# LayerNorm of a mixture-of-experts layer: a ring of four row tiles, gamma in PSUM, part of the gates on GpSimd

## The chip, the cores and the metric

The kernel runs on one core of one Trainium2 chip. A core has five engines that run side by side, each with its own instruction queue: TensorE (PE, matrix products, with weight loads shown as PEld), VectorE (DVE), ScalarE (ACT), GpSimd (POOL) and SyncE (SP, which here only issues DMAs). SBUF is the on-chip memory of 128 partitions, PSUM the small memory that TensorE writes. The metric is the device time of one execution in microseconds (us); the median of several runs is compared. A profile is the record of one execution.

## The reference

Two layers over images of 32 x 128 channels x 56 x 56, all in float32. The first is a depthwise 7x7 convolution, a LayerNorm over channels, and a mixture of 8 experts with top-2 routing and a capacity; the second is a coordinate attention with a 3x3 convolution. The diff touches the LayerNorm, the logits and the gates:

```python
x = conv_general_dilated(input, dw_kernel, ..., feature_group_count=C) + dw_bias
x = transpose(x, (0, 2, 3, 1))
mu = x.mean(-1, keepdims=True)
var = x.var(-1, keepdims=True)
x = (x - mu) / sqrt(var + 1e-06) * ln_gamma + ln_beta
xf = x.reshape(T, C)                       # T = 32*56*56 = 100352 tokens, C = 128
logits = xf @ Wg + bg                      # E = 8 experts
topv, topi = top_k(logits, 2)
wts = softmax(topv, axis=-1)
order = argsort(-wts[:, 0])                # a token's priority
# each expert takes at most CAP tokens, in that order; gelu MLP; two results per token, weighted
out1 = input + x_skip + layer_scale * moe_out
# second layer: coordinate attention, 3x3 convolution, SiLU
```

## The kernel before

The program runs in four stages, one after the other on the same core.

1. Depthwise convolution as banded matrix products (L165), written to the DRAM buffer `y_d`.
2. LayerNorm, logits, top-2 and gates (L194 to L349). This is the stage that the diff changes.
3. Routing per expert (a search for the threshold of the capacity, from L448 and L452 on, mostly DVE), then gather (L657), the expert's MLP (L678 to L688) and scatter (L717).
4. The second layer: combine (L973), attention, convolution (L1056 to L1068).

Stage 2 works on 16 pairs of images. A pair has 49 tiles of 128 tokens (`TPP = 49`), and is handled as two units: 24 tiles (h = 0) and 25 tiles (h = 1, `U = 25`). For a unit, `centre` (L293) does per group of three tiles: three matmuls with `proj`, which subtract the mean and also give 8 logit columns (L310, tile `lnps` in PSUM, a pool of 8), a copy of the 136 columns by ACT into the tile `cen` (L311, a pool of 4), and squares by ACT. Where a tile is squared alone (all of h = 0) the activation also sums it into `var` (L315, an activation and a read of the accumulator); otherwise three tiles are squared at once into `sqs` (L317, one buffer), and DVE sums them in one reduce (L322). `spread` (L319) makes `rstd` from `var` by two POOL instructions (L323, and the power L324). `normalise` (L326 on) scales each tile by `rstd` and gamma on DVE into the row tile `xn` (L331; 137 columns: 128 of the token, 8 gates, 1 mark; a pool of 2) and scales the logits (L333).

Once both units of a pair are there, `top` (L234) finds the two largest logits of each token by a chain of DVE instructions of 392 elements (L237 to L250) and two small ones (L251, L252), `exp` (L254) is one ACT instruction, and `gates` (L257) makes w0 and w1 (L261 to L265), the gate columns of the row (L267 to L269), the mark (L270), and the priorities `prio` (L272, L274), all on DVE; then SP issues the store of the whole row tile, 3.36 MB, to `acc_d` (L276). The same queue issues the load of the next pair's `lnyt` (L298, two buffers).

In the source the stage is a loop over k (L337 to L349): unit k is centred while unit k-2 is normalised, and the pair two behind gets its `top` (odd k) or `exp` and `gates` (even k). A scheduler then sets the order of each engine's instructions; dependencies between engines become semaphore waits. Stage 3 begins on DVE with L452, which reads `prio`, and ACT's queue issues a fill of part of `acc_d` with zeros (L648, four DMAs of 13.4 MB).

Of the kernel before, what the change touches and what calls it, by code (L numbers as in the profile page):

```python
# [21 lines left out]
E = 8  # L22
CAP = int(1.25 * T / E)
FF = 4 * C
P = 128
# [22 lines left out]
def moe_conv_then_coordatt_kernel(ctx: ExitStack, tc: tile.TileContext, a: dict, out: bass.AP):  # L48
# [145 lines left out]
    with ExitStack() as st:  # L194
# [3 lines left out]
        xp = st.enter_context(tc.tile_pool(name="lnx", bufs=2, reuse_waits="tile"))  # L198
        sp = st.enter_context(tc.tile_pool(name="lns", bufs=3, reuse_waits="tile"))
        pp = st.enter_context(tc.tile_pool(name="lnp", bufs=8, space=PSUM))  # L200
        halves = ((0, TPP // 2), (TPP // 2, TPP))
        U = TPP - TPP // 2
        NSQ = TPP // 2
# [17 lines left out]
        class Pair:  # L221
# [5 lines left out]
            def tile(self, pool, tag, shape=None):  # L227
                return pool.tile(shape or [P, TPP], F32, tag=tag, name=f"{tag}{self.i}", bufs=2 if pool is xp else 1)

            def open(self):  # L230
                self.row = self.tile(xp, "xn", [P, TPP, RW])
                self.l = self.tile(sp, "lgs", [P, TPP, E])

            def top(self):  # L234
# [4 lines left out]
                self.oh = [self.tile(sp, f"oh{k}", [P, TPP, E]) for k in range(2)]  # L239
# [17 lines left out]
            def gates(self):  # L257

                n, mx, w0, w1 = TPP, self.m[1], self.tile(sp, "w0"), self.tile(sp, "w1")
                t = self.tile(sp, "gt", [P, TPP, E])  # L260
# [6 lines left out]
                nc.vector.tensor_tensor(row[:, :, C : C + E], oh[0], over_experts(w0, n), ALU.mult)  # L267
                nc.vector.tensor_tensor(t, oh[1], over_experts(w1, n), ALU.mult)
                nc.vector.tensor_tensor(row[:, :, C : C + E], row[:, :, C : C + E], t, ALU.add)  # L269
                nc.vector.scalar_tensor_tensor(row[:, :, C + E : RW], self.later.unsqueeze(2), -1.0, all_e.unsqueeze(2),  # L270
                                               ALU.mult, ALU.add)
                nc.vector.tensor_tensor(oh[1], oh[0], oh[1], ALU.add)  # L272
                cols = slice(self.i * TPP, (self.i + 1) * TPP)
                nc.vector.tensor_tensor(prio[:, :, cols].rearrange("p e t -> p t e"), oh[1], over_experts(w0, n), ALU.mult)  # L274
# [5 lines left out]
        class Unit:  # L280
# [12 lines left out]
            def centre(self):  # L293
# [7 lines left out]
                self.cen = self.tile(cp1, "cen", [P, U, C + E])  # L301
                self.var = self.tile(sp, "var")
                self.alone = 0 if self.h else NSQ
                if self.alone < self.n:
                    self.sq = qp.tile([P, U, C], F32, tag="sqs", name=f"sqs{self.nm}")
                for g in range(0, self.n, 3):
# [4 lines left out]
                    nc.scalar.copy(self.cen[:, g : g + m, :], ps[:, 0:m, :])  # L311
                    if g < self.alone:
                        for j in range(m):
                            sq = sp.tile([P, C], F32, tag="sq", name=f"sq{self.nm}_{g}_{j}", bufs=1)
                            nc.scalar.activation(sq, ps[:, j, 0:C], AF.Square, accum_out=self.var[:, g + j : g + j + 1])  # L315
                    else:
                        nc.scalar.activation(self.sq[:, g : g + m, :], ps[:, 0:m, 0:C], AF.Square)  # L317

            def spread(self):  # L319
                self.rstd = self.tile(sp, "rstd")  # L320
                if self.alone < self.n:
                    nc.vector.tensor_reduce(self.var, self.sq[:, 0 : self.n], AX.X, ALU.add)  # L322
                nc.gpsimd.tensor_scalar(self.var, self.var, 1.0 / C, 1e-6, ALU.mult, ALU.add)  # L323
                nc.gpsimd.tensor_tensor(self.rstd, self.var, bc(mhalf, [P, self.n]), ALU.pow)  # L324

            def normalise(self):  # L326
                pair = pairs[self.i]
                if self.h == 0:
                    pair.open()
                for j in range(self.n):  # L330
                    nc.vector.scalar_tensor_tensor(pair.row[:, self.j0 + j, 0:C], self.cen[:, j, 0:C],  # L331
                                                   self.rstd[:, j : j + 1], gamma_bc, ALU.mult, ALU.mult)
                nc.vector.tensor_tensor(pair.l[:, self.j0 : self.j1, :], self.cen[:, :, C : C + E],  # L333
                                        over_experts(self.rstd, self.n), ALU.mult)

        units = [Unit(i, h) for i in range(NPAIR) for h in range(2)]
        for k in range(len(units) + 3):  # L337

            pair = pairs[(k - 3) // 2] if k >= 3 else None
            if k < len(units):  # L340
                units[k].centre()
            if pair and k % 2 == 0:
                pair.exp()
            if k < len(units):
                units[k].spread()
            if 2 <= k <= len(units) + 1:
                units[k - 2].normalise()
            if pair:
                (pair.top if k % 2 else pair.gates)()  # L349
# [801 lines left out]
```

## Time and profile before

| what | time |
|---|---|
| median of 5 runs | 4330.45 us (4323.46 to 4344.73) |
| the profiled execution's own time | 4335.32 us |
| its span, first to last instruction | 4333.6 us |
| stage 1, until the last write of `yt` (L181) | about 613 us |
| stage 2, first matmul of L310 to the end of the last L274 | 632.3 to 1107.1 us |
| stage 3, first L452 to the last scatter of L717 | 1107.1 to 3134 us |
| busy over the whole span: PE, DVE, ACT, POOL | 3473.2, 2528.5, 1446.2, 2763.9 us |

The stores of L276 show the rhythm of stage 2: they are issued at 705.03, 732.50, 759.95, 787.41, 814.88, 842.35, 869.81, 897.27, 924.73, 952.19, 979.64 and 1007.11 us, 27.46 or 27.47 us apart.

How to read the rows: a line such as "L331 DVE SCALAR_TENSOR_TENSOR xn<-cen,rstd,gamma_bc 128x128" names the line of the kernel, the engine, the operation, what is written from what, and the size (partitions x elements). Line numbers "before" are those of the listing above; the changed kernel has its own, a few higher.

### The profile page before, as it was taken

How to read it: one execution, taken by the hardware profiler on the slowest of the kernel's cores; microseconds unless marked ns; L12 is line 12 of the kernel's file. 1: busy time of each engine (PE TensorE's matmuls, PEld its weight loads, DVE VectorE, ACT ScalarE, POOL GpSimd, SP SyncE). 2: the span in 40 equal slices, each digit the busy share in tenths (PEclk: the TensorE clock that was granted, in tenths of full speed). 3: DMA queues.
4: the chain of work that ended last, by engine and by line, in shares of the span. 5: the costliest groups of instructions: out<-in, count | busy, mean ns of one | idle time of the engine just before them, and what ended most of it. 6: DMA issues, size and time to landing. Idle time of an engine off the chain costs nothing. (4 is left out here: it accounts for less than half of the span.)

```text
span 4333.6 us, 61146 instructions
## 1 busy us (share of the span) xinstructions
PE 3473.2 (80%) x21565; PEld 1960.5 (45%) x21565; DVE 2528.5 (58%) x5710; ACT 1446.2 (33%) x3123; POOL 2763.9 (64%) x2044
## 2 busy tenths in 40 slices
PE   7999979885068576678688669888769999999899
PEld 4644559885034232334343334444334444444444
DVE  3433328999948455775632112222268888888886
ACT  0000017664034343334344334445312333333332
POOL 5444414333048777677677567777779878787775
PEclk9999989776579787899899889999879999999999
DMA  9999985663991221111122122122165656555551
GB/s 177 177 178 183 191 171 213 246 246 157 320 297 43 51 62 46 51 44 53 51 56 57 50 55 57 57 57 57 53 220 163 201 166 196 181 186 188 166 165 72
DMA packets 678002, 580.88 MB, mean 134 GB/s; under 512 B 405848, under 2 KB 611184, under 8 KB 667248
## 3 DMA queue, kind: packets, MB, share of 16 engines
q1 hardware_dynamic: 411408, 319.81, 25.7%
q10 hardware_dynamic: 222816, 160.70, 14.3%
q0 software_dynamic: 43264, 94.64, 8.1%
q8 instruction: 184, 3.01, 0.3%
q14 instruction: 330, 2.70, 0.2%
HBM read 314.92 MB, written 260.09 MB: 133 GB/s over the span
## 5 line engine op out<-in xcount | busy, mean ns | idle before, releaser
L717 POOL DMA_INDIRECT acc_d<-yo,row x676 | 697.3, 1032 | 293.8 <-DMA acc_d<-yo,row 57.8
L1056 PE MATMUL pc<-v,wk 128*128 128x392 f32 x1920 | 702.7, 508 | 0.4 <-POOL v L1041 0.4
L678 PE MATMUL ph<-fxt,w 128*128 128x512 f32 (+1 forms) x1400 | 677.1, 627 | 5.7 <-ACT ht L679 5.7
L657 POOL DMA_INDIRECT xg_r<-acc_d,idx x556 | 560.5, 1008 | 182.8 <-issue 110.5
L686 PE MATMUL py<-ht,w 128*128 128x512 f32 (+1 forms) x1400 | 624.6, 589 | 0.0
L165 PE MATMUL acc<-xs,band 28*64 28x432 f32 (+2 forms) x11264 | 542.6, 532 | 59.2 <-issue 29.2
L679 ACT ACTIVATE ht<-ph,bias 128x512 f32<-128x512 f32 (+1 forms) x700 | 476.5, 682 | 246.0 <-PE ph L678 237.7
L1056 PEld LDWEIGHTS pc<-v,wk 128*128 128x128 f32 x1920 | 346.9, 191 | 306.9 <-issue 102.3
L165 PEld LDWEIGHTS acc<-xs,band 28*64 28x64 f32 x11264 | 311.7, 134 | 289.5 <-issue 193.8
L310 PE MATMUL lnps<-proj,lnyt 128*128 128x136 f32 x1568 | 364.8, 401 | 67.5 <-ACT sq L315 39.0
L678 PEld LDWEIGHTS ph<-fxt,w 128*128 128x128 f32 x1400 | 271.6, 205 | 296.9 <-issue 256.5
L310 PEld LDWEIGHTS lnps<-proj,lnyt 128*128 128x128 f32 x1568 | 350.8, 316 | 82.0 <-ACT sq L315 48.1
L686 PEld LDWEIGHTS py<-ht,w 128*128 128x128 f32 x1400 | 254.6, 190 | 261.1 <-issue 259.2
L712 DVE SCALAR_TENSOR_TENSOR yo<-pb,xg_r,yo 128x128 f32<-128x128 f32 (+1 forms) x568 | 160.3, 343 | 356.0 <-PE pb L695 339.8
L1036 POOL TENSOR_TENSOR d<-pad 128x3248 f32<-128x3248 f32 x32 | 227.6, 7113 | 156.4 <-DVE pad L1028 156.4
L1066 DVE SCALAR_TENSOR_TENSOR y<-pc,y 128x392 f32<-128x392 f32 x640 | 317.2, 552 | 14.7 <-PE pc L1056 14.7
L973 POOL TENSOR_TENSOR cxn<-cxn,cx 128x896 f32<-128x896 f32 x112 | 266.0, 2385 | 71.7 <-DMA cxn<-acc_d 26.3
L181 DVE TENSOR_TENSOR yt<-acc,m 128x448 f32<-128x448 f32 x256 | 146.4, 619 | 270.7 <-PE acc L165 177.5
L688 ACT ACTIVATE fyt<-py,b 128x512 f32<-128x512 f32 (+1 forms) x175 | 119.6, 683 | 505.4 <-PE py L686 393.3
L670 DVE COPY fxt<-pt 128x512 f32<-128x512 f32 (+1 forms) x175 | 119.4, 683 | 272.6 <-PE pt L668 271.3
L668 PE MATMUL pt<-ident,xg_r 128*128 128x128 f32 (+1 forms) x568 | 112.1, 311 | 198.1 <-DMA xg_r<-acc_d,idx 134.1
L709 ACT ACTIVATE yo<-xg_r,own 128x137 f32<-128x137 f32 (+1 forms) x568 | 194.8, 404 | 206.5 <-DVE own L705 140.8
(251 smaller groups left out, 4909.4 us busy)
## 6 DMA issues: line engine op xcount, KB each, us to landing
acc_d<-xn SPq DMA_DIRECT2D x16, 3356.5 KB
acc_d<-yo ACTq DMA_DIRECT2D x4, 13426.0 KB
lnyt<-y_d SPq DMA_DIRECT2D x16, 3136.0 KB
x<-in_x SPq DMA_DIRECT2D x16, 3136.0 KB
cxn<-acc_d SPq DMA_DIRECT2D x112, 448.0 KB
cx<-acc_d SPq DMA_DIRECT2D x112, 448.0 KB
out<-y ACTq DMA_DIRECT2D x64, 784.0 KB
xt<-in_x ACTq DMA_DIRECT2D x64, 392.0 KB
```

The costliest lines, as they stand in the source:

```text
L165: nc.tensor.matmul(acc[r][half * M : (half + 1) * M, :, lo:hi], lhsT=band[rows, t0 + o - least, 1 - par : 1 - par + M], rhs=xs[i][rows, ha ...
L310: nc.tensor.matmul(ps[:, j, :], lhsT=yf[:, self.j0 + g + j, :], rhs=proj, start=True, stop=True)
L657: d = nc.gpsimd.indirect_dma_start(out=xg[0:n, k, :], out_offset=None, in_=acc_d[0:T1, :], in_offset=bass.IndirectOffsetOnAxis(ap=idx[0][0 ...
L678: nc.tensor.matmul(ph[:, 0:N_], lhsT=w[0][:, f * P : (f + 1) * P], rhs=xt[:, 0:N_], start=True, stop=True)
L679: nc.scalar.activation(ht[:, f, 0:N_], ph[:, 0:N_], AF.Gelu, bias=w[2][:, f : f + 1])
L686: nc.tensor.matmul(py[:, 0:N_], lhsT=w2[:, f, :], rhs=ht[:, f, 0:N_], start=(f == 0), stop=(f == NF - 1))
L709: nc.scalar.activation(yo[0:n, k, :], xg[0:n, k, :], AF.Copy, scale=own[0:n, k : k + 1])
L717: d = nc.gpsimd.indirect_dma_start(out=acc_d[:, :], out_offset=bass.IndirectOffsetOnAxis(ap=row[0:n, k : k + 1], axis=0), in_=yo[0:n, k, : ...
L973: nc.gpsimd.tensor_tensor(xn, xn, x2, ALU.add)
L1036: nc.gpsimd.tensor_tensor(d, high, low, ALU.subtract)
L1056: nc.tensor.matmul(m[k], lhsT=wk[k][:, dw, :], rhs=v[:, k, rows, dw : dw + W], start=(dw == 0), stop=(dw == 2))
L1066: nc.vector.scalar_tensor_tensor(r[x], m[k], f, r[y_], ALU.mult, ALU.add)
```

## The change

- The row tile `xn` now comes from a ring of four and is opened in `centre`; ACT copies the matmul's 136 columns straight into it, and the scaling works in place. The tiles `cen` and the pool `lnx` are gone.
- Gamma is copied once into a PSUM tile `gamma_ps`, which the scaling reads; the pool of `lnps` has 7 tiles in place of 8.
- Of the second unit's 25 tiles, the first 6 are squared alone with a sum on ACT; `sqs` and the reduce cover 19.
- Five instructions of `gates` (the gate columns and `prio`) go from DVE to POOL, in another order; `oh0`, `oh1`, `w0` and `w1` have two buffers each.
- The logits' scaling is a method of its own. In the loop, `gates` comes first, then the logits of unit k-2, then `top` and `exp`, and the 24 or 25 scalings of unit k-2 come last.

```diff
@@ -195,12 +195,14 @@
         yp = st.enter_context(tc.tile_pool(name="lny", bufs=2, reuse_waits="tile"))
         cp1 = st.enter_context(tc.tile_pool(name="lnc", bufs=4, reuse_waits="tile"))
         qp = st.enter_context(tc.tile_pool(name="lnq", bufs=1, reuse_waits="tile"))
-        xp = st.enter_context(tc.tile_pool(name="lnx", bufs=2, reuse_waits="tile"))
         sp = st.enter_context(tc.tile_pool(name="lns", bufs=3, reuse_waits="tile"))
-        pp = st.enter_context(tc.tile_pool(name="lnp", bufs=8, space=PSUM))
+        pp = st.enter_context(tc.tile_pool(name="lnp", bufs=7, space=PSUM))
+        gp = st.enter_context(tc.tile_pool(name="lng", bufs=1, space=PSUM))
+        gamma_ps = gp.tile([P, C], F32, name="gamma_ps")
+        nc.vector.tensor_copy(gamma_ps, gamma_bc)
         halves = ((0, TPP // 2), (TPP // 2, TPP))
         U = TPP - TPP // 2
-        NSQ = TPP // 2
+        NSQ, NALONE = TPP // 2, 6
         rank_e = sp.tile([P, E], F32, name="rank_e", bufs=1)
         for e in range(E):
             nc.gpsimd.memset(rank_e[:, e : e + 1], float(E - e))
@@ -224,19 +226,18 @@
             def __init__(self, i):
                 self.i = i

-            def tile(self, pool, tag, shape=None):
-                return pool.tile(shape or [P, TPP], F32, tag=tag, name=f"{tag}{self.i}", bufs=2 if pool is xp else 1)
+            def tile(self, pool, tag, shape=None, bufs=1):
+                return pool.tile(shape or [P, TPP], F32, tag=tag, name=f"{tag}{self.i}", bufs=bufs)

             def open(self):
-                self.row = self.tile(xp, "xn", [P, TPP, RW])
-                self.l = self.tile(sp, "lgs", [P, TPP, E])
+                self.row = self.tile(cp1, "xn", [P, TPP, RW], 4)

             def top(self):

                 l, n = self.l, TPP
                 nc.vector.tensor_tensor(l, l, over_tokens(logit_c, n), ALU.add)
                 t = self.tile(sp, "gt", [P, TPP, E])
-                self.oh = [self.tile(sp, f"oh{k}", [P, TPP, E]) for k in range(2)]
+                self.oh = [self.tile(sp, f"oh{k}", [P, TPP, E], 2) for k in range(2)]
                 self.m = [self.tile(sp, f"m{k}") for k in range(2)]
                 self.later, second = self.tile(sp, "later"), self.tile(sp, "second")
                 for k in range(2):
@@ -256,22 +257,21 @@

             def gates(self):

-                n, mx, w0, w1 = TPP, self.m[1], self.tile(sp, "w0"), self.tile(sp, "w1")
-                t = self.tile(sp, "gt", [P, TPP, E])
+                n, mx, w0, w1 = TPP, self.m[1], self.tile(sp, "w0", None, 2), self.tile(sp, "w1", None, 2)
                 nc.vector.tensor_tensor(mx, mx, one_t, ALU.min)
                 nc.vector.tensor_tensor(w0, mx, one_t, ALU.add)
                 nc.vector.reciprocal(w0, w0)
                 nc.vector.scalar_tensor_tensor(w0, w0, 0.5, one_t, ALU.max, ALU.min)
                 nc.vector.tensor_tensor(w1, mx, w0, ALU.mult)
                 row, oh = self.row, self.oh
-                nc.vector.tensor_tensor(row[:, :, C : C + E], oh[0], over_experts(w0, n), ALU.mult)
-                nc.vector.tensor_tensor(t, oh[1], over_experts(w1, n), ALU.mult)
-                nc.vector.tensor_tensor(row[:, :, C : C + E], row[:, :, C : C + E], t, ALU.add)
                 nc.vector.scalar_tensor_tensor(row[:, :, C + E : RW], self.later.unsqueeze(2), -1.0, all_e.unsqueeze(2),
                                                ALU.mult, ALU.add)
-                nc.vector.tensor_tensor(oh[1], oh[0], oh[1], ALU.add)
+                nc.gpsimd.tensor_tensor(row[:, :, C : C + E], oh[0], over_experts(w0, n), ALU.mult)
+                nc.gpsimd.tensor_tensor(oh[0], oh[0], oh[1], ALU.add)
                 cols = slice(self.i * TPP, (self.i + 1) * TPP)
-                nc.vector.tensor_tensor(prio[:, :, cols].rearrange("p e t -> p t e"), oh[1], over_experts(w0, n), ALU.mult)
+                nc.gpsimd.tensor_tensor(prio[:, :, cols].rearrange("p e t -> p t e"), oh[0], over_experts(w0, n), ALU.mult)
+                nc.gpsimd.tensor_tensor(oh[1], oh[1], over_experts(w1, n), ALU.mult)
+                nc.gpsimd.tensor_tensor(row[:, :, C : C + E], row[:, :, C : C + E], oh[1], ALU.add)
                 rows = slice(self.i * TPP * P, (self.i + 1) * TPP * P)
                 nc.sync.dma_start(acc_d[rows, :].rearrange("(p j) c -> p j c", p=P), row)

@@ -298,40 +298,45 @@
                         nc.sync.dma_start(yt, y_d[2 * i : 2 * i + 2].rearrange("n c f -> c n f"))
                         yts[i] = yt.rearrange("c n f -> c (n f)").rearrange("c (p j) -> c j p", j=TPP)
                 yf = yts[self.i]
-                self.cen = self.tile(cp1, "cen", [P, U, C + E])
+                if self.h == 0:
+                    pairs[self.i].open()
+                self.cen = pairs[self.i].row[:, self.j0 : self.j1, :]
                 self.var = self.tile(sp, "var")
-                self.alone = 0 if self.h else NSQ
+                self.alone = NALONE if self.h else NSQ
                 if self.alone < self.n:
-                    self.sq = qp.tile([P, U, C], F32, tag="sqs", name=f"sqs{self.nm}")
+                    self.sq = qp.tile([P, U - NALONE, C], F32, tag="sqs", name=f"sqs{self.nm}")
                 for g in range(0, self.n, 3):
                     m = min(3, self.n - g)
                     ps = pp.tile([P, 3, C + E], F32, tag="ps", name=f"lnps{self.nm}_{g}")
                     for j in range(m):
                         nc.tensor.matmul(ps[:, j, :], lhsT=yf[:, self.j0 + g + j, :], rhs=proj, start=True, stop=True)
-                    nc.scalar.copy(self.cen[:, g : g + m, :], ps[:, 0:m, :])
+                    nc.scalar.copy(self.cen[:, g : g + m, 0 : C + E], ps[:, 0:m, :])
                     if g < self.alone:
                         for j in range(m):
                             sq = sp.tile([P, C], F32, tag="sq", name=f"sq{self.nm}_{g}_{j}", bufs=1)
                             nc.scalar.activation(sq, ps[:, j, 0:C], AF.Square, accum_out=self.var[:, g + j : g + j + 1])
                     else:
-                        nc.scalar.activation(self.sq[:, g : g + m, :], ps[:, 0:m, 0:C], AF.Square)
+                        nc.scalar.activation(self.sq[:, g - self.alone : g - self.alone + m, :], ps[:, 0:m, 0:C], AF.Square)

             def spread(self):
                 self.rstd = self.tile(sp, "rstd")
                 if self.alone < self.n:
-                    nc.vector.tensor_reduce(self.var, self.sq[:, 0 : self.n], AX.X, ALU.add)
+                    nc.vector.tensor_reduce(self.var[:, self.alone :], self.sq[:, 0 : self.n - self.alone], AX.X, ALU.add)
                 nc.gpsimd.tensor_scalar(self.var, self.var, 1.0 / C, 1e-6, ALU.mult, ALU.add)
                 nc.gpsimd.tensor_tensor(self.rstd, self.var, bc(mhalf, [P, self.n]), ALU.pow)

+            def logits(self):
+                pair = pairs[self.i]
+                if self.h == 0:
+                    pair.l = pair.tile(sp, "lgs", [P, TPP, E])
+                nc.vector.tensor_tensor(pair.l[:, self.j0 : self.j1, :], self.cen[:, :, C : C + E],
+                                        over_experts(self.rstd, self.n), ALU.mult)
+
             def normalise(self):
                 pair = pairs[self.i]
-                if self.h == 0:
-                    pair.open()
                 for j in range(self.n):
                     nc.vector.scalar_tensor_tensor(pair.row[:, self.j0 + j, 0:C], self.cen[:, j, 0:C],
-                                                   self.rstd[:, j : j + 1], gamma_bc, ALU.mult, ALU.mult)
-                nc.vector.tensor_tensor(pair.l[:, self.j0 : self.j1, :], self.cen[:, :, C : C + E],
-                                        over_experts(self.rstd, self.n), ALU.mult)
+                                                   self.rstd[:, j : j + 1], gamma_ps, ALU.mult, ALU.mult)

         units = [Unit(i, h) for i in range(NPAIR) for h in range(2)]
         for k in range(len(units) + 3):
@@ -339,14 +344,17 @@
             pair = pairs[(k - 3) // 2] if k >= 3 else None
             if k < len(units):
                 units[k].centre()
+                units[k].spread()
             if pair and k % 2 == 0:
+                pair.gates()
+            scaled = units[k - 2] if 2 <= k <= len(units) + 1 else None
+            if scaled:
+                scaled.logits()
+            if pair and k % 2:
+                pair.top()
                 pair.exp()
-            if k < len(units):
-                units[k].spread()
-            if 2 <= k <= len(units) + 1:
-                units[k - 2].normalise()
-            if pair:
-                (pair.top if k % 2 else pair.gates)()
+            if scaled:
+                scaled.normalise()


     with ExitStack() as st:
```

## The prediction

> **What bounds the kernel now.** I read the busy time by stretch first. The page's chain of waits covers only the last stage (its shares add up to some 30% of the span), so it says nothing of the stage that the diff touches; that one runs from the first matmul of L310 at 632.3 us to the last write of prio by L274, which ends at 1107.1 us. Columns: length, then busy time and count of PE, PEld, DVE, ACT and POOL, granted clock, DMA share, GB/s.
>
> ```profile
> 700.00:800.00 100.00, 90.75 (x396) 87.81 (x396) 98.64 (x275) 70.89 (x292) 44.16 (x17) 0.92 0.67 271
> 800.00:900.00 100.00, 84.11 (x354) 79.61 (x353) 98.97 (x283) 64.83 (x274) 36.92 (x14) 0.74 0.57 233
> 900.00:1000.00 100.00, 86.48 (x367) 82.22 (x366) 98.63 (x286) 63.75 (x258) 38.63 (x14) 0.81 0.64 258
> ```
>
> DVE is busy 99% of it, so DVE's work sets the pace; PE stands close behind it at 84 to 91%. The waits of 700 to 1000 us agree: ACT and POOL wait for DVE, and DVE for others 3.1 us in all.
>
> ```profile
> POOL var L323 <- DVE var L322: 127.0, 10, 13.0
> ACT cen L311 <- DVE lgs L333: 85.4, 20, 6.9
> ...
> DVE var L322 <- ACT sqs L317: 3.1, 1, 3.1
> ```
>
> The timeline of one pair (two images, 49 token tiles) gives the prices. Columns: start, length, engine, line.
>
> ```profile
> 808.62 3.48 DVE L322 TENSOR_REDUCE var<-sqs 128x25 f32<-128x3200 f32 x1
> ...
> 822.68 0.56 DVE L243 TENSOR_REDUCE m<-lgs 128x49 f32<-128x392 f32 x1
> ...
> 823.28 0.57 DVE L244 TENSOR_TENSOR gt<-lgs,m 128x392 f32<-128x392 f32 x1
> ...
> 829.41 6.12 DVE L331 SCALAR_TENSOR_TENSOR xn<-cen,rstd,gamma_bc 128x128 f32<-128x128 f32 x23
> ...
> 836.09 3.48 DVE L322 TENSOR_REDUCE var<-sqs 128x25 f32<-128x3200 f32 x1
> ```
>
> From reduce to reduce a pair takes 836.09 - 808.62 = 27.47 us. Prices are distances between starts, since neighbours overlap by a pipeline's depth: a scaling of L331 costs (6.12 - 0.34) / 22 = 0.263, so 49 cost 12.9; the reduce 3.39 (the next DVE start is 812.01); the top-two search 7.33 from L237 to the end of L252 less one scaling in it, 7.07; the gates 3.6; the two logits 0.67. Sum 27.6, the period.
>
> **The change, part by part (per pair, on DVE).**
>
> Five gate operations leave DVE (L267, L268, L269, L272: 0.47 to 0.48 each; L274: 816.18 - 815.51 = 0.67): -2.57.
>
> Six more tokens of each second half are squared with an accumulator on ACT, so the reduce has 19 instead of 25: 3.39 x 6/25 = -0.81.
>
> The logits come ahead of the scalings, so each step of the search has a scaling behind it. Today each step waits for the one before (822.68 to 823.28 is 0.60). The trace shows the other way too, in the first pair: from L237 at 681.59 to the scaling after L252 at 690.15 there are 8.56 us with 12 scalings among the steps; 8.56 - 12 x 0.263 = 5.41. So -1.66.
>
> Gamma read from PSUM: before has no scaling with that operand second. The nearest row is L712, the same operation and size with PSUM first and a pointer scalar; four in a row at 2003.32 take 1.12, which is (1.12 - 0.34) / 3 = 0.26 each, and its length is that of L331:
>
> ```profile
> L712 DVE SCALAR_TENSOR_TENSOR yo<-pb,xg_r,yo x568: 329/343/353, 1291.7 to 3122.3; 128x128 f32<-128x128 f32 x189, 64x128 f32<-64x128 f32 x1
> ...
> 2003.32 1.12 DVE L712 SCALAR_TENSOR_TENSOR yo<-pb,xg_r,yo 128x128 f32<-128x128 f32 x4
> ```
>
> I take 0, bounds -0.5 to +0.5 per pair (0.01 each way on 49).
>
> [...]
>
> The five operations on GpSimd have no row of 392 elements. The nearest are these (length in ns after the comma):
>
> ```profile
> L324 POOL TENSOR_TENSOR rstd<-var,mhalf 128x25 f32<-128x25 f32 x16 | 69.3, 4329 | 1.3
> ...
> L144 POOL TENSOR_TENSOR band<-hk 128x228 f32<-128x228 f32 x32 | 21.5, 670 | 111.4 <-PE acc L165 108.0 <-DMA hk<-in_dw_kernel 3.4
> ...
> L737 POOL TENSOR_TENSOR w<-w,ls_bc 128x512 f32<-128x512 f32 x8 | 10.2, 1269 | 34.4 <-PE ph L678 12.1 <-PE pb L740 6.6 <-PE pb L695 6.5
> ```
>
> So 0.67 to 1.27 each; by size I take 1.0, 5 us a pair, on top of two powers of 4.3 and their small partners: some 14.5 of POOL's period, no bound. What it costs DVE is a lock. At 1100.7 POOL ran two such products, and each DVE operation with two SBUF inputs that met one lasted until POOL was through (L252 0.20 elsewhere, L270 0.24):
>
> ```profile
> 1100.70 2.57 POOL L737 TENSOR_TENSOR w<-w,ls_bc 128x512 f32<-128x512 f32 x2 [3.27 <-DMA w<-in_W]
> ...
> 1100.74 1.28 DVE L252 TENSOR_TENSOR later<-later,second 128x49 f32<-128x49 f32 x1
> ...
> 1102.07 1.30 DVE L270 SCALAR_TENSOR_TENSOR xn<-later,all_e 128x49 f32<-128x49 f32 x1
> ```
>
> In the changed program POOL's first gate product starts at the clamp of w0 (new L264), and one scaling later DVE has w1 (new L265, two SBUF inputs): it stands about 0.7. Behind it come 22 scalings (5.8 us, one SBUF tensor each) and the reduce (2.6), 8.4 us that cover the other four products; one of them may still reach the logits or the search. I take +1.0, bounds 0 to 2.
>
> Sum: 27.47 - 2.57 - 0.81 - 1.66 + 1.0 = 23.4 us a pair.
>
> **What is late next.** ACT: its first half takes 808.42 to 820.2, 11.8; its second 822.13 to 828.98, 6.85; six more squares at 0.40 less two groups at 0.38 add 1.64: 20.3. PE: 184 matmul records in the 40 us from 660 to 700, at clock 1.00, are 0.217 each, 98 a pair: 21.3. Both stay under 23.4, narrowly, and one PSUM buffer fewer (seven of three tokens) leaves PE 21 tokens ahead. The ring adds a new wait: ACT may copy pair p+4 only once the store of pair p has landed. Issue to landing is about 8.2 us today:
>
> ```profile
> 814.00:816.00 2.00, 2.00 (x9) 1.74 (x8) 2.00 (x6) 1.84 (x11) 2.00 (x1) 0.50 0.50 215
> 816.00:818.00 2.00, 2.00 (x10) 2.00 (x10) 2.00 (x8) 1.84 (x11) 0.80 (x1) 0.50 1.01 430
> ...
> 822.00:824.00 2.00, 1.41 (x6) 1.01 (x5) 1.86 (x5) 1.87 (x5) 1.92 (x2) 1.00 0.54 228
> ```
>
> (issue at 814.88, the DMA idle from about 823). Behind the waiting copy stand ACT's squares and the exponential of pair p+1, on which DVE's gates wait; and on POOL the last gate product of pair p+1 is queued behind the variance of pair p+4's first half. So a loop: store 8.2, ACT 11.8, variance 0.2, product 1.0, and hand-overs, 21.5 to 22.5 us a pair. It fits under 23.4 with one microsecond to spare.
>
> **The end of the stage pays something back.** The last pair's prio is made by three POOL products instead of DVE. Before, the weight loads were issued at 1093 to 1096 and the last store at 1105.8; now the loads stand behind that store on SP's queue, and DVE's b2e (L639 new, among the first counting steps of the routing) and the bias wait for them. Store 8.2, more as the fill of acc_d shares the DMA, then 1 MB of weights: they land 14 to 20 us after the last gates, where the routing would have been at its third step, about 8. Constants of the routing, made on POOL under the scalings before, follow as well. Between 4 (only the fill counts, which starts later by that) and 16; I take 9. Filling the pipeline: 2.
>
> Sum: 16 x (27.47 - 23.4) - 9 - 2 = 54 us. The profiled span of 4333.6 becomes about 4280; the profiled run itself took 4335.32, and the median of the runs is 4330.45, so 4276.
>
> **Rivals.** (1) PE takes over. ACT's grouped squares hold all seven PSUM tiles until DVE's reduce of the pair before frees their buffer; PE then stops some 2 us per pair, and after a stop its clock stands at 0.50 (812 to 818 above). At the rate of 800 to 900, 84.11 / 354 = 0.238, 98 records are 23.3, plus 2: 25.3 a pair, gain 35 - 11 = 24, 4306. For it: PE's 84 to 91%. Against: its idle time today comes from DVE's hold on cen, which goes.
> (2) The gates come back as waits. If all five products block DVE for their 1.0, 22.4 + 5 = 27.4; the period gains nothing and the end costs 11: 4341, slower. It decides from about 4.3 us of standing a pair on. For it: L252 above. Against: the scalings behind them, and L1066, which also reads one PSUM and one SBUF tensor, keeps 543 to 568 ns throughout although POOL is busy beside it.
> (3) The ring becomes serial: each store waits in the queue for a load (9.3 us, 823.81 to 833.1). Then 8.2 + 9.3 + 11.8 + 2 = 31.3 a pair, 61 + 11 us slower: 4402. It decides once a store lands later than some 14 us after the last product. Against: the program has store p ahead of load p+4.
>
> **How the numbers follow.** Forecast 0.62, (1) 0.25, (2) 0.08, (3) 0.05. The forecast's own range, with the stall at 0 and the end at 4, or at 2 and 16, is 4256 to 4300; gamma's bounds move both ends by 8, of which I add half below, and (1) ends at 4306: 4252 to 4308. A run here tells about 0.3%, 13 us, from no change. Faster: the forecast and 0.23 of (1), 0.85; the same: the rest of (1) and half of (2), which lies 11 us above, 0.06; slower: the other half and (3), 0.09.
>
> **What would show it.** Right: starts of the reduce about 23.4 us apart, scalings still 0.26 apart, DVE over 95% busy, L265 at 0.7 to 1.0, ACT waiting a few us a pair on a store, a gap on DVE before b2e. Wrong: reduces 25 or more apart with DVE waiting for the exponential or rstd (1, 3), DVE operations of 392 elements above 1 us (2), or scalings 0.33 apart.

## The result, and the profile after

The changed kernel takes 4345.44 us (median of 52 runs, 4325.24 to 4376.64), the kernel before 4333.58 us (94 runs, 4313.03 to 4359.16): a ratio of 1.0029, 95% interval 1.0020 to 1.0038. It is slower by some 12 us. Forecast were 54 us less.

The profiled execution has a span of 4330.1 us and hides this, because its first stage happened to be 9 us shorter (the first matmul of the LayerNorm stage comes at 623.1 us, before at 632.3). Counted from that matmul, the last pair's store is issued after 482.8 us (before: 473.5) and the zero fill of `acc_d` after 485.2 us (before: 475.5). So the stage is 9.7 us longer, which is about what the medians say. All comparisons of stages below start at that matmul.

The busy time by stretch, with columns as before (length; busy time and count of PE, PEld, DVE, ACT, POOL; granted clock, DMA share, GB/s):

```profile
700.00:800.00 100.00, 88.19 (x380) 84.73 (x381) 78.36 (x238) 76.31 (x335) 47.36 (x30) 0.87 0.52 208
800.00:900.00 100.00, 84.75 (x355) 79.64 (x354) 80.82 (x257) 68.52 (x300) 51.54 (x32) 0.79 0.62 245
900.00:1000.00 100.00, 84.69 (x353) 79.69 (x353) 86.79 (x264) 69.13 (x298) 50.71 (x31) 0.78 0.60 237
```

DVE, 99% busy before, now has 13 to 22% idle time. No other engine took its place: PE is at 85 to 88%, ACT at 69 to 76%, POOL at about half. When nobody is busy all the time, the bound is a closed loop of waits. The waits of 700 to 1000 us (waiting engine, tile and line; what it waited for; us in total, times, longest) show where its links are:

```profile
POOL var L325 <- ACT sq L317: 82.0, 11, 14.0
DVE m L261 <- ACT m L256: 54.0, 10, 11.4
ACT xn L313 <- PE lnps L312: 48.3, 102, 4.9
...
PE lnps L312 <- ACT sq L317: 35.5, 43, 0.9
ACT xn L313 <- DMA acc_d<-xn: 29.0, 6, 6.0
```

DVE's gates wait for the exponential on ACT; ACT waits for PE, PE for ACT, and ACT for a store. Before, DVE waited 3.1 us in the same stretch. The timeline of one pair (start, length, engine, line; in brackets the idle time before and what ended it) puts them in order:

```profile
793.20 0.99 POOL L274 TENSOR_TENSOR xn<-xn,oh 128x392 f32<-128x392 f32 x1
...
794.22 0.33 SPq L276 DMA_DIRECT2D acc_d<-xn  x1
...
804.70 0.50 ACT L313 COPY xn<-lnps 128x408 f32<-128x408 f32 x1 [4.45 <-DMA acc_d<-xn]
...
811.27 3.08 PE L312 MATMUL lnps<-proj,lnyt 128*128 128x136 f32 x12 [0.86 <-ACT sq L317]
...
813.03 0.50 ACT L313 COPY xn<-lnps 128x408 f32<-128x408 f32 x1 [0.61 <-PE lnps L312]
...
815.21 2.91 PE L312 MATMUL lnps<-proj,lnyt 128*128 128x136 f32 x12 [0.86 <-ACT sq L317]
...
816.84 0.50 ACT L313 COPY xn<-lnps 128x408 f32<-128x408 f32 x1 [0.48 <-PE lnps L312]
...
820.22 0.21 POOL L325 TENSOR_SCALAR var<-var 128x24 f32<-128x24 f32 x1 [5.68 <-ACT sq L317]
820.51 1.35 POOL L274 TENSOR_TENSOR xn<-xn,oh 128x392 f32<-128x392 f32 x1
821.88 0.33 SPq L276 DMA_DIRECT2D acc_d<-xn  x1
```

From store to store it is 821.88 - 794.22 = 27.66 us, in four links. The store lands and ACT makes the first copy into the freed ring tile: 10.48. ACT goes through the first half of the pair that is being written, until POOL has all its sums of squares: 15.52. The variance, which POOL's queue holds ahead of the last gate product of an earlier pair (the one whose store comes next): 0.29. That product, and the store again: 1.37. Inside the second link ACT and PE stop for each other: PE writes two tiles (12 records), stands 0.86 us until ACT's squares free a PSUM tile, and ACT's copies wait for PE.

Why ACT's copies wait for PE is seen in ACT's queue. C is a copy, S a square, the first figure the half of the pair, the second the group of three tokens, EXP the exponential of an earlier pair; an extract of one pair each:

```
before  C0.6 S0.2 C0.7 S0.2 S0.2 S0.3 S0.3 S0.3 S0.4 ... S0.7 S0.7 S0.7 C1.0 S1.0 C1.1 S1.1 ... C1.8 S1.8
after   C0.6 EXP S0.2 C0.7 S0.2 C1.0 S0.2 S0.3 S0.3 S0.3 C1.1 S0.4 S0.4 C1.2 S0.4 S0.5 S0.5 S0.5 C1.3 S0.6 ...
```

Before, a second half's copies stood behind all squares of the first half. Now the scheduler has put them between the squares; that the copies no longer wait for a `cen` buffer of their own, since one row tile serves both halves, is the likely reason. With seven PSUM tiles, C1.0 needs a tile that S0.1 has freed and that PE has still to fill: in the pair above PE begins to fill it 0.17 us after that square, and the copy begins 0.04 us after PE is through.

Steps between stores, in us (the kernel before: 27.5 each, at the end 24.3 and 19.5):

```
after   41.9 24.1 41.5 27.7 27.6 29.4 28.0 27.7 27.7 27.7 27.8 27.7 19.6 19.8 21.1
```

The last three steps, in which no pair of the ring has to wait any more, take 20 us. No later pair is centred beside them, and before the last step took 19.5 as well, so they do not show by themselves that the work had become shorter.

### The profile page after: what moved, and what is told of

Same layout as the page of the kernel before. It is cut to its first block, busy times and chain, and to the rows that moved or that the text cites. A ratio compares the mean times of both kernels' runs of the same rounds, so it can differ in the third digit from the quotient of the medians.

```text
span 4330.1 us, 61297 instructions
## 1 busy us (share of the span) xinstructions
PE 3474.9 (80%) x21565; PEld 1965.3 (45%) x21565; DVE 2461.0 (57%) x5631; ACT 1469.4 (34%) x3283; POOL 2811.4 (65%) x2124
## 5 line engine op out<-in xcount | busy, mean ns | idle before, releaser
L725 POOL DMA_INDIRECT acc_d<-yo,row x676 | 684.9, 1013 | 277.6 <-DMA acc_d<-yo,row 67.3
```

Source lines behind the costliest of these rows:

```text
L725: d = nc.gpsimd.indirect_dma_start(out=acc_d[:, :], out_offset=bass.IndirectOffsetOnAxis(ap=row[0:n, k : k + 1], axis=0), in_=yo[0:n, k, : ...
```

## The experiments

Two theories stood at the start. A: the ring's loop through POOL's queue is the bound. B: ACT and PE, handing seven PSUM tiles to each other, need some 27 us by themselves. The runs were made on other chips, on which the kernel before takes 4805 to 4830 us; there the expert stage takes 2333 to 2379 us instead of 1848, while the stage studied here agrees (the changed kernel: 485.7 us against 485.2). So each ratio is against the kernel before on the same chip, and the stage is read from the profiles:

| run | between stores | first matmul to fill | first matmul to first scatter | time against before (95%) |
|---|---|---|---|---|
| before (first profile) | 27.5 | 475.5 | 656.2 | 1 |
| e0_after | 27.6 to 29.3 | 485.7 | 664.0 | 1.0042 (1.0022 to 1.0062) |
| e1_pool_order | 27.5 to 27.8 | 482.6 | 668.1 | 1.0044 (1.0015 to 1.0074) |
| e2_act_halves | 28.0 to 29.0 | 468.4 | 651.1 | 1.0011 (0.9986 to 1.0036) |
| e3_gamma_sbuf | 20.7, 33.3 in turn | 469.8 | 654.8 | 1.0006 (0.9977 to 1.0036) |
| e4_loads_act | 27.0 to 28.9 | 485.6 | 676.2 | 1.0090 (1.0059 to 1.0120) |
| e5_both | 22.9 to 24.0 | 430.2 | 607.6 | 0.9946 (0.9920 to 0.9972) |
| e6_exp_first | 23.6 | 423.0 | 598.8 | 0.9923 (0.9895 to 0.9952) |
| e8_before_fill | 30.4 | - | 651.7 | 1.0027 (1.0004 to 1.0050) |
| e9_exp_gamma_sbuf | 24.4 | 433.1 | 618.6 | 0.9910 (0.9884 to 0.9935) |
| e10_squares_back | 23.5 | 422.9 | 608.4 | 0.9900 (0.9866 to 0.9933) |
| e11_last_store_act | 23.6 | 423.1 | 600.4 | 0.9890 (0.9839 to 0.9941) |
| e12_quarter_fill | 23.6 | - | 575.0 | 0.9846 (0.9796 to 0.9897) |

One row is one profile; the times have 4 to 10 runs a kernel. The steps are those of the steady part. The first scatter waits for a fill that the last part of this section describes; where all of it stands behind the stage it takes 169 to 180 us from its first packet to its last, so differences of some 10 us in that column need not come from the stage.

**The changed kernel beside the others.**

> The changed kernel itself, beside the others of this call, so that all stand against one chip: stores 27.7 us apart in the steady part, stage from first matmul to fill 485 us, 1.002 to 1.004 of the kernel before. Both theories say the same of it.

As expected, the time within its interval. It is the yardstick for the rest.

**The last gate product ahead of the variance.** `order(a, b)` only fixes that a comes behind b in an engine's queue; it adds no wait.

```diff
+                self.last = nc.gpsimd.tensor_tensor(row[:, :, C : C + E], row[:, :, C : C + E], oh[1], ALU.add)
...
+                var = nc.gpsimd.tensor_scalar(self.var, self.var, 1.0 / C, 1e-6, ALU.mult, ALU.add)
+                if self.h == 0 and self.i >= 3:
+                    order(var.ins, pairs[self.i - 3].last.ins)
```

> Theory A (the ring is the bound, because on POOL's queue the last gate product of pair p, and with it its store, stands behind the variance of pair p+3, whose rows ACT may only write once store p-1 has landed): with the product put ahead of that variance the loop is store 10.4 + seven copies 4.3 + exponential 0.4 + gates on DVE 1.5 + five products 5.0 = 21.6 us and no longer bounds; stores 23.5 to 25.5 us apart, the stage from first matmul to fill 435 to 455 us instead of 485, time 4300 to 4318. Theory B (ACT and PE hand seven PSUM tiles back and forth and need some 27 us a pair by themselves, the ring wait is only where the slack shows): stores still 27 to 28 apart, time 4340 to 4350.

B's figure. ACT's wait for the store is gone from the waits altogether, so the ring's loop was opened, and the period stays. What remains are ACT and PE (waits of 800 to 1000 us, then the timeline):

```profile
ACT xn L317 <- PE lnps L316: 51.4, 110, 0.6
...
PE lnps L316 <- ACT sq L321: 24.0, 28, 0.9
```

```profile
867.10 3.02 PE L316 MATMUL lnps<-proj,lnyt 128*128 128x136 f32 x12 [0.86 <-ACT sq L321]
868.73 0.50 ACT L317 COPY xn<-lnps 128x408 f32<-128x408 f32 x1 [0.48 <-PE lnps L316]
870.15 0.50 ACT L317 COPY xn<-lnps 128x408 f32<-128x408 f32 x1 [0.26 <-PE lnps L316]
870.98 3.09 PE L316 MATMUL lnps<-proj,lnyt 128*128 128x136 f32 x12 [0.86 <-ACT sq L321]
```

In pair 8 each of the 17 copies begins 0.03 to 0.11 us after PE has filled its tile: ACT is never behind, and PE never ahead.

**The copies of a second half behind the squares of the first.**

```diff
+                    copy = nc.scalar.copy(self.cen[:, g : g + m, 0 : C + E], ps[:, 0:m, :])
+                    if self.h:
+                        order(copy.ins, units[2 * self.i].last.ins)
```

(`last` is here the unit's last square.)

> ACT's copies of a pair's second half are put behind all squares of its first half; POOL's queue stays as it is. Theory A: the loop keeps its shape but its ACT term falls from 15.4 to 11.9 us: 10.4 + 11.9 + 0.3 + 1.4 = 24.0; stores 24 to 25 us apart, stage 445 to 455, time 4303 to 4318. Theory B: the copies only move, PE still stops for the same seven tiles: 27 to 28 apart, time 4340 to 4350.

Neither figure, but for a reason that the profile shows. ACT's first half does fall to 11.9 us (pair 8: first copy at 815.75, last square done at 827.65), and the uneven first steps shrink from 41.9, 24.0, 41.7 to 31.4, 22.5, 28.0; the stage is 17 us shorter. But the scheduler answered by putting all five gate products of a pair, not one, behind the variance, and the store is waited for longer than ever (waits of 800 to 1000 us, then the timeline):

```profile
ACT xn L317 <- DMA acc_d<-xn: 62.3, 7, 9.7
```

```profile
856.80 0.21 POOL L331 TENSOR_SCALAR var<-var 128x24 f32<-128x24 f32 x1 [8.53 <-ACT sq L323]
857.09 0.87 POOL L273 TENSOR_TENSOR xn<-oh,w 128x392 f32<-128x392 f32 x1
...
861.05 1.19 POOL L278 TENSOR_TENSOR xn<-xn,oh 128x392 f32<-128x392 f32 x1
...
862.27 0.33 SPq L280 DMA_DIRECT2D acc_d<-xn  x1
...
873.80 0.50 ACT L317 COPY xn<-lnps 128x408 f32<-128x408 f32 x1 [9.65 <-DMA acc_d<-xn]
```

Store to copy 11.5, ACT 11.9, variance 0.3, five products 5.2: 28.9. This is A's loop, with other terms. So e2 did not take away the loop of ACT and PE alone: it also put four more products into the ring. With one product, as in the changed kernel, its terms would add up to an estimated 11.5 + 11.9 + 0.3 + 1.4 = 25.1; no run has that order by itself.

**Gamma back in SBUF, the eighth PSUM tile back.**

```diff
-        pp = st.enter_context(tc.tile_pool(name="lnp", bufs=7, space=PSUM))
+        pp = st.enter_context(tc.tile_pool(name="lnp", bufs=8, space=PSUM))
...
-                                                   self.rstd[:, j : j + 1], gamma_ps, ALU.mult, ALU.mult)
+                                                   self.rstd[:, j : j + 1], gamma_bc, ALU.mult, ALU.mult)
```

> Gamma back in SBUF, the eighth PSUM tile back. Theory A: PE gains one tile of three tokens, 1.4 us, on ACT: stores 25.5 to 27 apart, unless DVE's scalings, now with two SBUF tensors each, stand beside POOL's five products: then up to 5 x 0.9 more on DVE a pair, 27.9, and nothing is gained; time 4320 to 4350. Theory B: eight tiles end the handing back and forth: stores 24 to 25 apart, time 4300 to 4320, with scalings still 0.26 apart.

Steps of 20.7 and 33.3 in turn, 27.0 in the mean: within A's range, but by luck, since A's loop is not there, and against B as it was put. Here POOL's queue happens to hold the product ahead of the variance, ACT waits for a store once in 200 us (0.4 us), and PE and ACT still wait for each other (45.1 us in 98 waits). One tile more does not end that; the order of ACT's queue makes it. Why the steps alternate stayed open.

**Both orders together, and then the exponential ahead too.**

> Both edits of the first two runs together: the last gate product ahead of the variance on POOL, and ACT's copies of a second half behind the squares of the first. Theory AB (two closed loops of nearly the same length lie over each other, the ring through POOL's queue, and ACT with PE over seven PSUM tiles; each run before took away one and met the other): both are gone, what is left is DVE at 23.4, PE at 21.3 to 23.3 and ACT at 20.3, stores 23.4 to 25 us apart, stage 425 to 445 us against 485, time 1.2 to 0.8% below the changed kernel. Theory C (a third loop of 27 to 28 us, such as POOL's power waiting 5.4 us for a buffer of rstd until DVE's last scaling): stores 27 or more apart, stage 465 to 485.

The next run adds one more order, so that ACT's exponential of pair p stands ahead of all copies of pair p+3:

```diff
+                    elif self.i >= 3:
+                        order(copy.ins, pairs[self.i - 3].e.ins)
```

> As the run with both edits, and ACT's exponential of pair p ahead of all copies of pair p+3. Theory AB: nothing waits for the exponential any more; 0 to 0.5 us a pair less than with both edits, stage 420 to 445. If the exponential behind the ring's wait was the loop that matters (store 10.4 to 11.5, copies 4.3, exponential, gates 1.5, products 5.2: 22 to 23): no difference beyond 0.5 us a pair either, since that loop is shorter than DVE's 23.4. A kernel slower than with both edits would say that ACT now waits for DVE's search.

Theory AB holds. Two loops of nearly the same length lay over each other; opening the ring alone left the loop of ACT and PE (e1), repairing ACT's order alone left a ring, longer by what the scheduler added (e2), opening both takes 55 us off the stage, and the third edit 7 more. The kernel with all three is at 0.9923 of before, 1.2% below the changed kernel on the same chip. DVE and PE are both near full, at a clock of 0.93 instead of 0.76 to 0.79:

```profile
800.00:900.00 100.00, 95.45 (x420) 93.31 (x420) 97.83 (x309) 83.50 (x370) 57.04 (x38) 0.93 0.74 301
900.00:1000.00 100.00, 93.05 (x406) 90.52 (x405) 96.50 (x310) 83.84 (x363) 62.86 (x38) 0.93 0.57 235
```

**Single parts, with the orders repaired.** First gamma in SBUF with eight PSUM tiles (the edit of e3 on top of e6), then the six squares undone:

```diff
-        NSQ, NALONE = TPP // 2, 6
+        NSQ, NALONE = TPP // 2, 0
```

> The kernel with both edits and the exponential ahead, with gamma back in SBUF and an eighth PSUM tile. If POOL's products hold up DVE operations that read two tensors from SBUF (the scalings are such operations again): DVE's busy time was 31 us higher with gamma in SBUF in the earlier run, 2 us a pair, and up to five products of 0.9 can each hold one up: stores 25.5 to 28 us apart instead of 23.5, stage 450 to 485. If they don't: 23 to 23.6 apart, stage 415 to 423, since PE has one tile more.

> The kernel with both edits and the exponential ahead, without the six more squares on ACT: the reduce has 25 tokens again. If DVE is the bound there: 3.48 instead of 2.67 a reduce, 24.3 us a pair instead of 23.5, stage 434 to 438, 12 us slower than with the six squares. If ACT or PE is the bound (ACT has 1.6 us a pair less): 22.5 to 23.5, stage 410 to 423.

Gamma: 24.4 a pair with DVE busy 98.03 and 100.00 of 100 us (800 to 1000 us), below the 25.5 to 28 expected and above the other case. Its scalings, against those of the kernel with gamma in PSUM (line, then busy time and mean ns):

```profile
L345 DVE SCALAR_TENSOR_TENSOR xn<-xn,rstd,gamma_bc 128x128 f32<-128x128 f32 x784 | 248.9, 372 | 0.0
```

```profile
L348 DVE SCALAR_TENSOR_TENSOR xn<-xn,rstd,gamma_ps 128x128 f32<-128x128 f32 x784 | 219.9, 336 | 0.0
```

29.0 us over 16 pairs, 1.8 a pair; the longest takes 1162 ns instead of 346. Of the 784, 39 take more than 380 ns, and each of these has a POOL operation on tensors beside it; they make up 26 of the 29 us. So POOL's operations did hold up scalings with two tensors in SBUF here, 39 of 784, and with gamma in PSUM none was held up (346 ns at most). The pairs are only 0.8 us longer for it, since DVE is not full in e6, and the kernel's time does not show it (0.9910 against 0.9923). The squares: 23.5 a pair, with DVE busy 100.00 of 100 us in both stretches. The period is the same without them, so they are worth nothing here: with them DVE has some 0.6 us less to do, and PE (93 to 95% busy) and ACT, which waits for it, come out at the same 23.5; what a repair there would bring was not tried.

**The end of the stage, and the fill.** The profiles had shown something else: the changed kernel's routing is 14 us late (first gather at 1203.3 us against 1189.4), and yet the first scatter comes at 1289.2 against 1288.5 (times of the profiles themselves, in which the last store is issued at 1106.0 and 1105.8). POOL waits at the first scatter in both, here in the kernel before and then after:

```profile
POOL acc_d L717 <- DVE fxt L670: 41.1, 1, 41.1
```

```profile
POOL acc_d L725 <- DVE junk L456: 28.0, 1, 28.0
```

The releasers named had long been done; what ends then is the fill of `acc_d`, 55.0 MB that ACT issues at the end of the stage (four times the page's 13426 KB, of 1024 bytes each). Its last packet ends 1.5 to 1.6 us before the first scatter in both profiles. Four runs tried it. The loads of the first two experts' weights, and of the biases, issued by ACT:

```diff
-            nc.sync.dma_start(w1, a["W1"][e])
+            (nc.sync if e > 1 else nc.scalar).dma_start(w1, a["W1"][e])
...
```

> The weights and biases of the first two experts are issued by ACT instead of SP, so that they no longer stand behind the last store. If the end of the stage costs what the prediction said (9 us, paid in the routing): the third counting step 9 to 10 us earlier and the time 9 us less, 4336. If the fill of acc_d is what the next stage waits for (the first scatter comes at the same 1288.5 and 1289.2 us in both profiles, while the counting is 14 us apart): the counting is 9 to 10 us earlier, the first scatter stays at stage end + 181, and the time stays at 4340 to 4350.

The fill of the kernel before in 16 pieces, each behind a pair's store (the fill at the end of the stage is taken out):

```diff
+    def fill(k, store):
+        r0, n = T1 + k * T // NPAIR, T // NPAIR // P // ZB
+        z = nc.sync.dma_start(acc_d[r0 : r0 + T // NPAIR, :].rearrange("(p s t) c -> p s t c", p=P, t=ZB),
+                          bc(zr.unsqueeze(1), [P, n, ZB, RW]))
+        order(z.ins, store.ins)
...
+                fill(self.i, store)
```

> The kernel before, with one edit: the zeros of acc_d's second part are written in 16 pieces, each behind a pair's store on SP's queue, instead of all at the end of the stage by ACT. If the fill is what the next stage waits for (POOL stood 41.1 us before the first scatter in the profile of before): the first scatter comes some 40 us earlier after the stage's end, time 25 to 40 us less (0.5 to 0.8%), the stage itself still 27.5 a pair as DVE bounds it. If the fill is hidden: the first scatter moves, the time does not (within 0.3%).

The kernel with the repaired orders, with the last store issued by ACT:

```diff
-                nc.sync.dma_start(acc_d[rows, :].rearrange("(p j) c -> p j c", p=P), row)
+                (nc.scalar if self.i == NPAIR - 1 else nc.sync).dma_start(acc_d[rows, :].rearrange("(p j) c -> p j c", p=P), row)
```

> The kernel with both edits and the exponential ahead, with the last pair's store issued by ACT, so that SP's queue lets the weight loads go before it. Counting's third step 9 us earlier and the first gather 10 us earlier. If the fill decides the first scatter (176 us behind the fill's issue in the run without this edit): the scatter and the time stay, ratio 0.990 to 0.994. If the counting decides: scatter and time 9 to 10 us earlier, ratio 0.988 to 0.991.

And a quarter of the fill in four pieces on top of it (the rest stays at the end):

```diff
+FILL = (4, 7, 10, 13)
...
+                if self.i in FILL:
+                    fill(FILL.index(self.i), store)
...
-        for k in range(4):
+        for k in range(1, 4):
```

> As the run before it, and a quarter of the fill written in four pieces behind the stores of pairs 4, 7, 10 and 13. If the fill decides the first scatter: it ends 44 us earlier, then the way from the first gather to the first scatter decides (70 us where no fill stood in the way): scatter 10 to 20 us earlier than in the run before it, ratio 0.986 to 0.991, unless the four pieces (8 to 10 us of DMA each) make ACT wait for a store: up to 4 times 5 us back. If the fill does not decide: no difference or slower.

e4, beside e0: the third counting step comes 488.1 us after the first matmul instead of 497.0, the first gather 13 us earlier, the first scatter not earlier but 12 us later: only one of the four weight loads got ahead of the fill on ACT's queue, and POOL's scaling of the weights waited 39.5 us for them. The time is 1.0090 of before, with an interval that just meets that of e0. e8: a miss. The 16 pieces use the same DMA as the loads (busy 86% from 900 to 1000 us), pairs took up to 34.7 us and then 30.4 steadily, and the first scatter came only 4.5 us earlier; the time is 0.27% above before. What it does show is that with no fill behind the stage the first scatter follows the first gather by 70.2 us, before by 99.1. e11: gather 11 us earlier than in e6 (507.6 us after the first matmul against 518.2), POOL's wait at the scatter longer by about as much, and the scatter where it was; the time, 0.9890, lies within both cases. The wait in e6, then in e11:

```profile
POOL acc_d L735 <- DVE yo L730: 23.1, 1, 23.1
```

```profile
POOL acc_d L735 <- DVE row L724: 35.7, 1, 35.7
```

e12: with a quarter of the fill out of the way the scatter is 25 us earlier, POOL's waits there come to 13.1 us, and the pairs still take 23.6. It is the fastest version found, at 0.9846 (0.9796 to 0.9897) of before; its four runs (4751 to 4767 us) all lie below the four of e11 (4771 to 4800). The packets settle the matter: in every profile with the whole fill behind the stage except e4 its last packet ends 1.5 to 1.6 us before the first scatter, in e4 13.4, where the weights are waited for, and in e12 16.6. So the fill decides when the experts begin to write, as long as the routing is not slower than it.

## Why the prediction was wrong, point by point

**The step that failed** is the loop: "store 8.2, ACT 11.8, variance 0.2, product 1.0, and hand-overs, 21.5 to 22.5 us a pair. It fits under 23.4 with one microsecond to spare." Its links were named rightly and are the links of the trace; two were mis-sized. The store takes 10.5 us until ACT can write (11.5 in e2). The 8.2 was read from stretches of 2 us; by its packets even a store with nothing beside it takes 9.0 us from issue to its last packet (before, issue at 842.35), here it is 10.0, and ACT's copy begins 0.5 later. The load of the next pair is issued 3 us behind the store here and 8.9 behind it before; that its first packets make up the 1.0 is likely, but no run tried it by itself. ACT's half takes 15.5, because 11.8 was read from a queue order that the change itself dissolves. With 27.66 instead of 21.5 to 22.5 the loop lies above DVE's work, and the period is the loop's. A second step failed beside it: ACT's 20.3 and PE's 21.3 were added up one by one and found to "stay under 23.4, narrowly", and their handing back and forth of the PSUM tiles was put at nothing in the forecast; with the ring open it alone holds the pairs at 27.5 us (e1).

**Rival (1)** named ACT and PE over seven PSUM tiles, and was right that PE stops, though over 100 us its clock is no lower than before on the whole (0.87, 0.79 and 0.78 against 0.92, 0.74 and 0.81). It priced this at 25.3 us a pair; alone it costs 27.5 (e1). It blamed the grouped squares held until DVE's reduce; the copies set between the squares do it (e5 against e1), and eight tiles do not cure it (e3). Rival (2) did not come: no DVE operation of 392 elements took more than 0.85 us from 760 to 1030 us, and the scalings are still 0.26 apart. Rival (3) had the ring as the bound, but with the load ahead of the store and 31.3 us. The two mechanisms that came true were both in the text, each too small or in another form, and in the form that came neither had a case on the slower side.

**DVE's sum** of 23.4 us was nearly right. The gates (-2.57), the logits ahead (-1.66) and the reduce (-0.81; 2.68 instead of 3.48) came as costed in their sum: without the squares DVE, busy all the time, takes 23.5, where 27.47 - 2.57 - 1.66 = 23.24 leaves 0.3 for the locks and all else. L265 stood as foreseen (median 840 ns against 198 before), which is 0.64 a pair; hardly any other operation of the changed kernel did, so +1.0 for all locks was a little too much. In e6, with the orders repaired, L265's median is 204. With the squares DVE needs about 22.9 (97% of 23.55).

**Gamma at nothing**: right against the kernel before (335 ns in the median against 342). Scalings 0.33 apart, one of the signs that were to prove the prediction wrong, did not come: in the changed kernel 22 in a row took 5.76 us (811.64), 0.26 apart. What was missed is that gamma in SBUF would have cost 1.8 us a pair once POOL made the products (e9 against e6).

**The end of the stage** was put at 9 us. The routing is indeed later (DVE waits 9.1 us for b2e, the first gather comes 13.9 us later), but that lies under the fill, which starts 2.4 us after the last store instead of 2.0. What counted was 0.4 (the first scatter comes 183.2 us after the last store instead of 182.7). The prediction had this case as its lower bound of 4 and chose the other. **Filling** was put at a loss of 2; the first store comes 9.1 us earlier, but the next three steps take 107.5 us instead of 82.4 and lose more than that.

**The signs** that the prediction gave as proof against it are what came: the reduces 27.7 apart in the steady part and DVE waiting for the exponential. Over the 15 steps the stores need 419.2 us where 15 x 23.4 would be 351: 37 of the difference in the first three steps, 41 in the nine steady ones, 10 won back in the last three. With the two queue orders and the exponential put right, the stage is 52.5 us shorter than before and the first scatter 57.4 us earlier, close to the 54 that the sum had promised; the time, by the medians, falls by 36 us only, and where the rest goes was not looked into.

## What to carry to other kernels

When a bound engine gets faster, add up every loop that passes through a ring or a shared buffer, with terms read from the new program's queue order, not from the old trace: a buffer that is removed takes away waits that had kept a queue in a good order. If no engine is busy all the time and a repair of one loop changes nothing, look for a second loop of the same length before giving the first one up. And follow the stage's end to what the next stage really waits for: here a fill of 55.0 MB, not the counting that looked late.

## What the runs showed of the hardware

Stops of PE of less than a microsecond (0.86 us here) stood ahead of a halved granted clock. In the changed kernel's profile that clock changes only at steps of 3.41 us. Three such steps (columns as in the first view, PE busy behind the length, the granted clock third from the end):

```profile
808.13:811.55 3.42, 2.56 (x12) 2.36 (x12) 2.22 (x9) 3.15 (x15) 1.67 (x2) 1.00 0.99 421
811.55:814.96 3.41, 2.81 (x12) 2.48 (x12) 3.41 (x14) 2.51 (x13) 2.83 (x4) 0.50 0.01 4
814.96:818.37 3.41, 2.91 (x12) 2.71 (x12) 3.41 (x11) 2.65 (x14) 0.00 (x0) 1.00 0.02 5
```

PE is idle for 0.86 us of the first step, and the next has 0.50; it is idle for 0.60 of the second, and the next has 1.00, since the stop at 814.36, just as long, is cut in two by the step's end. Over the stage (121 steps) the line is sharp: each of the 46 steps with 0.69 us or more of PE idle was followed by 0.50, none of the 75 with less. In e6 it is the same with 10 and 94 steps; in the kernel before the line is less sharp (of 98 steps with less than 0.69, 18 were followed by 0.50). Over 100 us that made 0.78 to 0.87, against 0.93 with the repaired orders and the same 98 records a pair. A record took 0.239 us of PE's busy time in the changed kernel and 0.228 in e6 (800 to 1000 us), 1.1 us a pair, so the orders won twice. Here a step with 0.69 of its 3.41 us idle was enough for 0.50 in the next.

A scaling on DVE with both tensors in SBUF took up to 1162 ns beside POOL's operations on tensors (e9), against 346 at most with the second tensor in PSUM (e6 and the changed kernel). Not each POOL operation did this: in the kernel before, 126 scalings with both tensors in SBUF ran beside the power (L324) and took 355 at most.

The same kernel took 4330 us on one chip and 4805 to 4830 us on others. Of the changed kernel there are profiles of both kinds, 498 us apart, of which 485 lie between the first and the last scatter of the expert stage. The cause was not looked into.
